# A sequence model's scan layers on one core: the skip term, the norm's factor, the ffn's buffer and the place of z

## The chip, the cores and the metric

The kernel runs on one core of a Trainium2 chip. The metric is the device time of one execution in microseconds, here the median of three runs. Five engines work in parallel, each through its own instructions in order: TensorE (PE), VectorE (DVE), ScalarE (ACT), GpSimd (POOL) and SyncE (SP), which in this kernel only issues transfers (DMAs).

## The reference

Four parts follow one another on an image `x` of 2 x 128 x 64 x 64; the change touches only the first, two scan layers over the 4096 positions of each image, all in fp32:

```python
t = embed(x)
for i in range(2):
    r = t
    u, z = split(layernorm(t) @ in_w.T)              # 256 channels each
    u = silu(causal_conv4(u) + conv_b)
    dt, Bm, Cm = split(u @ xproj_w.T, [8, 24])       # 8, 16 and 16 wide
    dt = softplus(dt @ dt_w.T + dt_b)
    # for every position, in order:
    #   h = exp(dt * A) * h + (dt * u) * Bm          # 256 x 16 states
    #   y = sum over the 16 states of h * Cm
    y = (y + u * ssm_D) * silu(z)                    # u * ssm_D: the skip term
    t = y @ mout_w.T + r
    r = t
    t = gelu(layernorm(t) @ ffn_w1.T + b1) @ ffn_w2.T + b2 + r
x = x + outc(t)
```

`layernorm(t)` is `(t - mean) * rsqrt(var + eps) * ln_g + ln_b` over the 128 channels. After it come two attention layers and a layer of features at several scales, which are left as they are.

## The kernel before, in words

A piece (`items[i]`) is 512 positions of one image in one layer; there are 2 images x 2 layers x 8 = 32. Channels lie on the 128 partitions. The 256 x 16 states of a piece are worked in 8 groups of 4 scans: in a group (`g`), 128 partitions hold 32 channels x 4 states, and each of the four scans (`m`) is 128 x 512. A scan takes one slot, so a piece has 32 slots.

The order of all engines is written out by hand. `slot(i, todo, t_)` emits, for every slot, the work of the scan: transfers that spread `dt` to a group's partitions three groups ahead (`spread_dt`, tile `dtb`, on SP), a product that spreads `dt*u` (`spread_dtu`, tile `pdu` in a single PSUM buffer, PE), `y_pair` (the sum over states of two groups, 32 small products on PE into `py`), the `scan` itself (DVE, line 430), `decay` four scans ahead (`da = exp(dt*A)`, ACT, line 419, four PSUM buffers), and at a group's end `times_b` (DVE, line 412, which reads `pdu` and fills the next `h`) and on GpSimd the carry (line 432) and `h * Cm` (line 433, `cb`). After that the slot emits what `background(i)` has listed for it with `at(slot, function, ...)`. That is everything else, for neighbouring pieces: with `i` the piece that is scanned, `n = i + 1`, `p = i - 1`, `q = i - 2`, `r = i + 2`,

- `pu_taps` and `pu_out` (convolved u of `n`), `xproj`, `spread_bc` (Bm and Cm to all groups through DRAM, tiles `dr`, `bb`, `cb`), `dtproj`, `soft_plus` (`dt`), `dt_end` (`dtu = dt * u`, GpSimd, line 393);
- `pz_mm`, `pz_out` (z of `i`), and `silu` of u of `n` with z of `i` at slot 11;
- `y_out` (the skip term, DVE, line 453), `gate` (times z, GpSimd, line 456), `mix_out`, `mix_add`;
- the norm for two pieces at once, the ffn's of `p` and the mixer's of `r`: `ln_centre` and `ln_square` (slots 12 to 15), `ln_var` (17), on 2 x 512 values `ln_eps` (18), `ln_rs` (19: Ln, Exp and Square on ACT), `ln_newton` (20: GpSimd, then ACT, line 298) and `ln_step` (21: GpSimd, line 302, the factor `rs` is done), `ln_spread` (27: a product with a row of ones spreads `rs` to 128 partitions, `pr`, line 306), `ln_scale` (28: DVE, line 310) and `ln_shift` (29: ACT, line 323, into `x2` or `xn`);
- `ffn_up` (slots 30 and 31, `ph`, line 478, and `hid`, line 479), `gelu`, `ffn_down`, `ffn_add`, `out_mm`, `out_add`.

An engine takes its instructions strictly in this order; the PSUM pool `mm` of two buffers serves all products but `pdu`, `py` and `da`. Before the first piece is scanned, the loop runs for `i = -2` and `i = -1`, which prepare pieces 0 and 1, and `load_rest` and `fold_out` issue large transfers there. The `h` tiles come from a ring of five buffers, which `hid` shares:

```python
w["hid"] = sp.tile([P, 4, CH], F32, name="hid", tag="h", bufs=5)
```

## Time and profile before

| | |
|---|---|
| median of 3 runs (lowest, highest) | 4975.6 us (4974.84, 4981.31) |
| profiled execution: its own time, its span | 4975.69 us, 4973.9 us |
| layers (the change's place) | from the start to about 2100 us |
| mean clock of PE that was granted | 0.949 over the span; 0.90 from 278 to 2051 us |
| DVE busy in the layers, a 200 us window (400 to 600) | 187.7 us |
| PE, ACT, GpSimd busy in the same window | 183.2, 146.6, 145.3 us |
| `dtb` of one quarter, 64 KB, issue to landing | 2.0 us |
| `cb` and `bb`, 256 KB each, four in a row, issue to landing | 4.6 and 4.5 us |

The profile counts an engine as busy while an instruction of its own runs; a matmul's end is modelled. A timeline row gives the start, the time from the first instruction's start to the last one's end, engine, line, operation, output and inputs, how many instructions were merged, and in brackets the idle time before it with what ended it. A row of groups gives the count, busy time and mean of one in ns, and then the idle time before the group with its releasers. An fp32 product of 128 x 512 is two matmul instructions in the records (x2). A window's row has length, then busy time (and instructions) of PE, PE's weight loads, DVE, ACT and GpSimd, then the granted clock, DMA's busy share and GB/s.

### The profile page before, as it was taken

The numbers are of one execution on the slowest core, as the hardware profiler recorded it, in microseconds if no ns is written. First come the engines' busy times: TensorE is split into PE (matmuls) and PEld (weight loads), VectorE is DVE, ScalarE is ACT, GpSimd is POOL, SyncE is SP. The second block draws the span as 40 slices with busy tenths as digits, with TensorE's granted clock in tenths as the row PEclk, the third lists the DMA queues.
The fourth block names the chain that finished last, engine by engine and source line by source line (L and its number), as shares of the span: only waits on it lengthen the run. The fifth ranks groups of instructions, "written<-read, shape, count | busy, mean of one in ns | idle before, by whom it ended". The sixth has DMA issues, their size and how long they took to land.

```text
span 4973.9 us, 48435 instructions
## 1 busy us (share of the span) xinstructions
PE 4643.1 (93%) x14634; PEld 2218.0 (45%) x14634; DVE 3975.5 (80%) x4155; ACT 2361.8 (47%) x3225; POOL 2331.1 (47%) x1974
## 2 busy tenths in 40 slices
PE   6899999999988899899999999999999999999997
PEld 2222222222222222266667766666666666333332
DVE  6999999999999999878886677767766775667775
ACT  4677777777777777632222232233333332323332
POOL 3777776676777777613332233333333332334231
PEclk8888898988999989899999999999999999999998
DMA  6333332223333333214444444444444443000000
GB/s 163 68 67 68 69 69 67 67 67 71 69 69 69 71 73 71 69 36 126 113 111 123 113 109 115 122 99 111 114 101 98 114 112 83 3 7 7 7 5 9
DMA packets 242485, 386.28 MB, mean 78 GB/s; under 512 B 88608, under 2 KB 89136, under 8 KB 233776
## 3 DMA queue, kind: packets, MB, share of 16 engines
q1 hardware_dynamic: 193072, 316.01, 26.1%
q10 hardware_dynamic: 49152, 67.17, 5.4%
q8 instruction: 117, 1.92, 0.2%
q14 instruction: 144, 1.18, 0.1%
HBM read 101.09 MB, written 13.37 MB: 23 GB/s over the span
## 4 chain that ended last, share of the span: by engine, by line
PE 46%; POOL 25%; issue 12%; DVE 8%; DMA 4%; SPq 3%; ACT 3%; ACTq 0%; POOLq 0%; DVEq 0%
POOL h L433 19%; PE pq L780 13%; PE po L830 13%; DVE tr L810 3%; SPq L821 3%; DMA pt<-tr 3%; PE pa L677 2%; PE pf L1135 2%; PE pqkv L1162 2%; PE pw L1221 1%; POOL dtu L393 1%; POOL z L456 1%; PE pb L677 1%; PE pfus L1286 1%; PE psc L1186 1%
## 5 line engine op out<-in xcount | busy, mean ns | idle before, releaser
L817 POOL COPY pt<-tr 32x512 f32<-32x512 f32 x1024 | 644.7, 630 | 1410.8 <-DVE tr L810 700.7
L430 DVE TENSOR_TENSOR_SCAN h<-da,carry,h 128x512 f32<-128x512 f32 x1024 | 1241.6, 1265 | 65.1 <-ACT da L419 36.2
L433 POOL TENSOR_TENSOR h<-h,cb 128x2048 f32<-128x2048 f32 x256 | 1160.9, 4535 | 20.8
L780 PE MATMUL pq<-k,q 128*128 128x512 f32 x2048 | 963.4, 593 | 12.5 <-DVE sc L785 12.5
L830 PE MATMUL po<-pt,vt 128*128 128x256 f32 x4096 | 965.6, 379 | 3.5 <-POOL pt L817 3.5
L795 ACT ACTIVATE sc<-sc,nm 128x2048 f32<-128x2048 f32 x256 | 510.5, 1995 | 886.8 <-DVE nm L791 656.4
L830 PEld LDWEIGHTS po<-pt,vt 128*128 128x128 f32 x4096 | 777.9, 190 | 309.5 <-issue 227.5
L785 DVE TENSOR_SCALAR_CACHE_REDUCE sc<-pq 128x1024 f32<-128x1024 f32 x512 | 624.8, 1222 | 333.8 <-PE pq L780 311.7
L419 ACT ACTIVATE da<-dtb,am 128x512 f32<-128x512 f32 x1024 | 681.4, 684 | 221.3 <-DVE h L430 205.6
L412 DVE TENSOR_TENSOR h<-bb,pdu 128x2048 f32<-128x2048 f32 x256 | 581.4, 2271 | 85.4 <-PE py L445 28.3
L810 DVE STREAM_TRANSPOSE tr<-sc 128x2048 f32<-128x2048 f32 x256 | 591.6, 2311 | 65.7 <-DMA pt<-tr 59.3
L445 PE MATMUL py<-h,sel 128*32 128x512 f32 x2048 | 513.6, 645 | 1.8 <-POOL h L433 1.8
L780 PEld LDWEIGHTS pq<-k,q 128*128 128x128 f32 x2048 | 382.2, 190 | 291.5 <-issue 247.4
L406 PE MATMUL pdu<-dtu,fsel 128*128 128x512 f32 x512 | 327.8, 727 | 99.5 <-DVE h L412 97.5
L445 PEld LDWEIGHTS py<-h,sel 128*32 128x32 f32 x2048 | 115.6, 118 | 418.7 <-issue 413.1
L333 PE MATMUL pu<-xn,wu 128*128 128x512 f32 x512 | 245.9, 614 | 10.0 <-ACT u L339 8.3
L406 PEld LDWEIGHTS pdu<-dtu,fsel 128*128 128x128 f32 x512 | 96.6, 215 | 307.4 <-DVE h L412 180.5
L432 POOL COPY carry<-h 128x4 f32<-128x4 f32 x256 | 47.8, 187 | 390.3 <-DVE h L430 386.2
L1228 DVE TENSOR_TENSOR ov<-v,pw 128x2048 f32<-128x2048 f32 x64 | 146.2, 2284 | 65.1 <-PE pw L1221 65.1
L1162 PE MATMUL pqkv<-f,ws 128*128 128x512 f32 x384 | 188.8, 617 | 3.0 <-DVE prod L1179 2.3
L1232 POOL TENSOR_TENSOR ov<-ov 128x2048 f32<-128x2048 f32 x16 | 72.6, 4536 | 237.0 <-DVE ov L1228 237.0
L393 POOL TENSOR_TENSOR dtu<-dt,u 128x1024 f32<-128x1024 f32 x32 | 75.1, 2348 | 199.1 <-ACT dt L387 199.1
(265 smaller groups left out, 5152.4 us busy)
## 6 DMA issues: line engine op xcount, KB each, us to landing
pt<-tr SPq DMA_DIRECT2D x2048, 64.0 KB, 2.0
dtb<-dt SPq DMA_DIRECT2D x1024, 64.0 KB, 2.0
pt<-tr ACTq DMA_DIRECT2D x1024, 64.0 KB, 2.1
bb<-dr SPq DMA_DIRECT2D x128, 256.0 KB, 4.5
cb<-dr SPq DMA_DIRECT2D x128, 256.0 KB, 4.6
uw<-ufold SPq DMA_DIRECT2D x12, 576.0 KB, 4.4
uw<-dkept SPq DMA_DIRECT2D x20, 288.0 KB, 3.1
xt<-in_x SPq DMA_DIRECT2D x16, 256.0 KB, 4.8
```

The source lines that it names most:

```text
L406: nc.tensor.matmul(pdu, lhsT=four(s_ % 4), rhs=st[i]["dtu"][:, s_ // 4, :], start=True, stop=True)
L412: nc.vector.tensor_tensor(h, st[i]["bc", 0], pdu.unsqueeze(1).to_broadcast([P, 4, CH]), ALU.mult)
L419: nc.scalar.activation(da, st[i]["dtb", s_], AF.Exp, scale=am[items[i][1]][:, j, gg, m : m + 1])
L430: nc.vector.tensor_tensor_scan(h[:, m, :], da, h[:, m, :], carries[b, l][:, j, gg, m : m + 1], ALU.mult, ALU.add)
L433: nc.gpsimd.tensor_tensor(h, h, st[i]["bc", 1], ALU.mult)
L445: nc.tensor.matmul(py[r : r + 32, :], lhsT=sel, rhs=st[i]["h", s_ + k][:, m, :], start=(m == 0), stop=(m == 3), tile_position=(0, r),)
L780: nc.tensor.matmul(pq[:, i, :], lhsT=sta["q", r, grp][:, it * P : (it + 1) * P], rhs=sta["k"][:, at : at + CH], start=True, stop=True)
L785: nc.vector.tensor_scalar(dst, pq, 1.0, None, ALU.mult, ALU.max, accum_out=sta["mx"][:, c2 : c2 + 1])
L795: nc.scalar.activation(sc, sc, AF.Exp, bias=nm, scale=scale, accum_out=sm[:, hh : hh + 1])
L810: nc.vector.transpose(tr, sta.pop(("sc", r, blk, hh)).rearrange("p (t r f) -> p r t f", r=NB, f=32))
L817: nc.gpsimd.tensor_copy(dst, src)
L830: nc.tensor.matmul(sta["po", r, grp], lhsT=sta["vt"][:, jt, :], rhs=rhs, start=(jt == 0), stop=(jt == N // P - 1))
```

## The change

1. The skip term becomes a product: `turn_skip` builds `ssm_D` as a diagonal matrix on GpSimd (at each new image and layer), `y_pair` starts the sum in `py` with it, and `y_out` is a copy on ACT.
2. The norm's factor: `ln_eps` joins `ln_rs`, `ln_step` joins `ln_newton`, both a slot earlier; `ve` and `nt` lie in rows of `sq`. The product that spread `rs` is replaced by a transfer to DRAM (`ln_out`, slot 21) and a broadcast transfer into `sq` (`ln_in`, slot 23), both on SP; `ln_scale` runs on GpSimd (slots 25 and 27), `ln_g` moves into `ln_shift` (slot 28).
3. `hid` has a buffer of its own outside the ring of `h`, and `xr` uses the buffer of `x2`.
4. z is computed a piece ahead, for `n` at slots 24 to 27 rather than for `i` at slots 1 to 6.

```diff
-        def ln_eps(w, n):
-            w["ve"] = spl.tile([2, CH], F32, name="ve", tag="ve")
-            nc.scalar.activation(w["ve"][:n], w.pop("var")[:n], AF.Identity, bias=eps[:n])
-
         def ln_rs(w, n):
-            w["rs"] = spl.tile([2, CH], F32, name="rs", tag="rs")
-            nc.scalar.activation(w["rs"][:n], w["ve"][:n], AF.Ln)
...
+            ve, nt = w["sq"][:n, 0, :], w["sq"][:n, 1, :]
+            rs = w["rs"] = spl.tile([2, CH], F32, name="rs", tag="rs")
+            nc.scalar.activation(ve, w.pop("var")[:n], AF.Identity, bias=eps[:n])
+            nc.scalar.activation(rs[:n], ve, AF.Ln)
+            nc.scalar.activation(rs[:n], rs[:n], AF.Exp, scale=-0.5)
+            nc.scalar.activation(nt, rs[:n], AF.Square)
 
         def ln_newton(w, n):
 
-            nt = w["nt"][:n]
-            nc.gpsimd.tensor_tensor(nt, nt, w["ve"][:n], ALU.mult)
+            ve, nt, rs = w["sq"][:n, 0, :], w["sq"][:n, 1, :], w["rs"][:n]
+            nc.gpsimd.tensor_tensor(nt, nt, ve, ALU.mult)
             nc.scalar.activation(nt, nt, AF.Identity, bias=c15[:n], scale=-0.5)
-
-        def ln_step(w, n):
-            rs = w["rs"][:n]
-            nc.gpsimd.tensor_tensor(rs, rs, w["nt"][:n], ALU.mult)
-
-        def ln_spread(w, k, n):
-            w["pr", k] = mmt("pr")
-            nc.tensor.matmul(w["pr", k], lhsT=pick(k, n), rhs=w["rs"][:n], start=True, stop=True)
-
-        def ln_scale(w, k, i):
+            nc.gpsimd.tensor_tensor(rs, rs, nt, ALU.mult)
+
+        def ln_out(w, n):
+            w["rd"] = dp.tile([2, CH], F32, name="rd", tag="rd")
+            nc.sync.dma_start(w["rd"][:n], w["rs"][:n])
+
+        def ln_in(w, n):
+            src = w["rd"][:n].rearrange("(o k) f -> o (k f)", o=1)
+            nc.sync.dma_start(w["sq"][:, :n, :].rearrange("p k f -> p (k f)"), src.to_broadcast([P, n * CH]))
+
+        def ln_scale(w, k):
             cen = w["cen"][:, k, :]
-            nc.vector.scalar_tensor_tensor(cen, cen, vl("ln_g", i), w.pop(("pr", k)), ALU.mult, ALU.mult)
+            nc.gpsimd.tensor_tensor(cen, cen, w["sq"][:, k, :], ALU.mult)
...
-            nc.scalar.activation(dst, w["cen"][:, k, :], AF.Identity, bias=vl("ln_b", i))
+            nc.scalar.activation(dst, w["cen"][:, k, :], AF.Identity, bias=vl("ln_b", i), scale=vl("ln_g", i))
...
-                st[i]["py", j] = yp.tile([P, CH], F32, name="py", tag="y")
+                py = st[i]["py", j] = yp.tile([P, CH], F32, name="py", tag="y")
+                nc.tensor.matmul(py, lhsT=skip["now"][:, j, :], rhs=st[i]["u"][:, j, :], start=True, stop=False)
...
+        def turn_skip(i):
+            if items[i][2] == 0:
+                dg = skip["now"] = wp.tile([P, NJ, P], F32, name="skip", tag="skip")
+                for j in range(NJ):
+                    nc.gpsimd.tensor_tensor(dg[:, j, :], ident, vl("ssm_D", i, j).to_broadcast([P, P]), ALU.mult)
+
         def y_out(i, j):
-            u = st[i]["u"][:, j, :]
-            nc.vector.scalar_tensor_tensor(u, u, vl("ssm_D", i, j), st[i].pop(("py", j)), ALU.mult, ALU.add)
+            nc.scalar.copy(st[i]["u"][:, j, :], st[i].pop(("py", j)))
...
-                if i == NI - 1:
-                    w["hid"] = spa.tile([P, 4, CH], F32, name="hid", tag="sc", bufs=3)
-                else:
-                    w["hid"] = sp.tile([P, 4, CH], F32, name="hid", tag="h", bufs=5)
+                w["hid"] = spl.tile([P, 4, CH], F32, name="hid", tag="hid")
...
-                xr = st[i]["xr"] = spl.tile([P, CH], F32, name="xr", tag="xr")
+                xr = st[i]["xr"] = spl.tile([P, CH], F32, name="xr", tag="x2")
...
+                at(24, pz_mm, n, 0), at(25, pz_out, n, 0)
+                at(26, pz_mm, n, 1), at(27, pz_out, n, 1)
             if has(i):
-                at(1, pz_mm, i, 0), at(3, pz_out, i, 0)
-                at(5, pz_mm, i, 1), at(6, pz_out, i, 1)
+                at(2, turn_skip, i)
...
-                at(27, ln_spread, w, k, m), at(28, ln_scale, w, k, it)
-                at(29, ln_shift, w, k, it, second)
+                at(25 + 2 * k, ln_scale, w, k)
+                at(28, ln_shift, w, k, it, second)
             if pair:
-                at(17, ln_var, w, m), at(18, ln_eps, w, m), at(19, ln_rs, w, m), at(20, ln_newton, w, m), at(21, ln_step, w, m)
+                at(17, ln_var, w, m), at(18, ln_rs, w, m), at(19, ln_newton, w, m)
+                at(21, ln_out, w, m), at(23, ln_in, w, m)
```

More of the change, by code (lines that the diff above doesn't have):

```diff
@@ L144, in tile_conv_seq @@
         load_x(0, 0)
-        wl, wu, wd, am, cws = [], [], [], [], []
+        wl, wu, wd, am, cws, skip = [], [], [], [], [], {}
         def load_layer(l):
@@ L281, in ln_var @@
                 nc.tensor.matmul(var[:n], lhsT=kc[:, at : at + n], rhs=w["sq"][:, k, :], start=(k == 0), stop=(k == n - 1))
-        def ln_eps(w, n):
-            w["ve"] = spl.tile([2, CH], F32, name="ve", tag="ve")
-            nc.scalar.activation(w["ve"][:n], w.pop("var")[:n], AF.Identity, bias=eps[:n])
         def ln_rs(w, n):
-            w["rs"] = spl.tile([2, CH], F32, name="rs", tag="rs")
-            nc.scalar.activation(w["rs"][:n], w["ve"][:n], AF.Ln)
-            nc.scalar.activation(w["rs"][:n], w["rs"][:n], AF.Exp, scale=-0.5)
-            w["nt"] = spl.tile([2, CH], F32, name="nt", tag="nt")
-            nc.scalar.activation(w["nt"][:n], w["rs"][:n], AF.Square)
+            ve, nt = w["sq"][:n, 0, :], w["sq"][:n, 1, :]
@@ L445, in y_pair @@
                     nc.tensor.matmul(
-                        py[r : r + 32, :], lhsT=sel, rhs=st[i]["h", s_ + k][:, m, :], start=(m == 0), stop=(m == 3),
+                        py[r : r + 32, :], lhsT=sel, rhs=st[i]["h", s_ + k][:, m, :], start=False, stop=(m == 3),
                         tile_position=(0, r),
                     )
+        def turn_skip(i):
[3 more added lines that the diff above has]
+                    nc.gpsimd.tensor_tensor(dg[:, j, :], ident, vl("ssm_D", i, j).to_broadcast([P, P]), ALU.mult)
         def y_out(i, j):
-            u = st[i]["u"][:, j, :]
-            nc.vector.scalar_tensor_tensor(u, u, vl("ssm_D", i, j), st[i].pop(("py", j)), ALU.mult, ALU.add)
+            nc.scalar.copy(st[i]["u"][:, j, :], st[i].pop(("py", j)))
         def gate(i):
```

## The prediction

> **What bounds the kernel now.** I read the page first: engine shares, then the slices.

> ```profile
> PE 4643.1 (93%) x14634; PEld 2218.0 (45%) x14634; DVE 3975.5 (80%) x4155; ACT 2361.8 (47%) x3225; POOL 2331.1 (47%) x1974
> DVE  6999999999999999878886677767766775667775
> PEclk8888898988999989899999999999999999999998
> ```

> The layers fill the first 17 slices; only there does the change act. DVE is full and PE looks full at a clock below one, so neither is yet the answer. I then took 28 whole pieces (from one start of `gate`, line 456, to the 28th after it) by windows, and DVE's groups in that stretch.

> ```profile
> 278.24:2051.38 1773.14, 1609.90 (x4088) 489.76 (x4087) 1650.43 (x1232) 1303.93 (x1840) 1256.55 (x591) 0.90 0.31 70
> ```

> ```profile
> L430 DVE TENSOR_TENSOR_SCAN h<-da,carry,h 128x512 f32<-128x512 f32 x897 | 1087.6, 1265 | 51.7 <-ACT da L419 25.8 <-POOL carry L428 3.6 <-ACT hid L479 1.5
> L412 DVE TENSOR_TENSOR h<-bb,pdu 128x2048 f32<-128x2048 f32 x224 | 508.8, 2271 | 71.0 <-PE py L445 26.3 <-PE pdu L406 19.7 <-issue 13.0
> L453 DVE SCALAR_TENSOR_TENSOR u<-u,vec,py 128x512 f32<-128x512 f32 x56 | 41.0, 732 | 0.0
> L310 DVE SCALAR_TENSOR_TENSOR cen<-cen,vec,pr 128x512 f32<-128x512 f32 x55 | 38.0, 730 | 0.0
> ```

> A piece takes 1773.14/28 = 63.3 us: DVE works 58.9 (57.0 in scan and product, 2.8 in the two steps that leave, less overlap) and waits 4.4. That invites "2.8 off DVE, 2.8 off the piece". The timeline of one piece (735 to 799 us) says otherwise. PE:

> ```profile
> 745.94 1.13 PE L406 MATMUL pdu<-dtu,fsel 128*128 128x512 f32 x2
> 748.93 3.62 PE L306 MATMUL pr<-rs,kc 2*128 2x512 f32 x4 [1.86 <-POOL rs L302]
> 754.02 2.07 PE L406 MATMUL pdu<-dtu,fsel 128*128 128x512 f32 x2 [1.47 <-DVE h L412]
> 756.02 5.27 PE L445 MATMUL py<-h,sel 128*32 128x512 f32 x16
> 761.23 3.89 PE L478 MATMUL ph<-x,wl 128*128 128x512 f32 x8
> ```

> From `pdu` of slot 28 (691.1 in the piece before, 754.0 in this one) to `pdu` of slot 16 (ended 735.5) PE runs 44.4 us without a gap, and DVE waits for it there. From 735.5 to 754.0 (18.5 us) PE waits, and a chain through ACT, GpSimd and DVE sets the time. The piece is the sum of the two. GpSimd, ACT and SP in that second part, and a small transfer's time to land (the last figure of its row):

> ```profile
> 738.47 2.35 POOL L393 TENSOR_TENSOR dtu<-dt,u 128x1024 f32<-128x1024 f32 x1 [5.47 <-ACT dt L387]
> 741.03 4.54 POOL L433 TENSOR_TENSOR h<-h,cb 128x2048 f32<-128x2048 f32 x1
> 745.54 1.26 POOL L297 TENSOR_TENSOR nt<-nt,ve 2x512 f32<-2x512 f32 x1
> 747.63 1.25 POOL L302 TENSOR_TENSOR rs<-rs,nt 2x512 f32<-2x512 f32 x1 [0.83 <-ACT nt L298]
> 749.09 4.51 POOL L433 TENSOR_TENSOR h<-h,cb 128x2048 f32<-128x2048 f32 x1
> 753.82 4.53 POOL L433 TENSOR_TENSOR h<-h,cb 128x2048 f32<-128x2048 f32 x1
> ```

> ```profile
> 746.83 0.72 ACT L298 ACTIVATE nt<-nt,c 2x512 f32<-2x512 f32 x1 [2.61 <-POOL nt L297]
> 747.46 3.88 ACT L419 ACTIVATE da<-dtb,am 128x512 f32<-128x512 f32 x6
> ```

> ```profile
> 742.18 1.92 SPq L377 DMA_DIRECT2D cb<-dr  x4
> ```

> ```profile
> dr<-dbl SPq DMA_DIRECT2D x20, 64.0 KB, 1.6
> ```

> GpSimd runs 738.5 to 758.3 with one gap of 0.8 us: it is full exactly where the change gives it two more products.

> **The change, part by part** (us of one piece; D = 738.4, when `dt` is done; the lines are those of the kernel before).

> *Skip term, its sum to ACT.* Off DVE: two of 0.73. On PE: two products of 0.86 to 0.95 at full clock, like a `pdu`. The one at slot 12 (with groups 0, 1) lies in PE's full stretch: +0.9. The one at slot 28 falls where the windows show the clock at 0.51 (749 to 756) and 0.58 (756 to 760), where one `pdu` takes 2.07: +0.9 to +1.9. ACT gets two copies of 0.59 in gaps of its own: `py` is finished before them (745.9, against 747.46 and later). The diagonal is built four times in all, two small products on GpSimd in a gap of over 2 us: 0, or some 3 us in all without the gap. `gate` now waits for ACT's copy where it waited for DVE's step: 0.

> *z a piece ahead.* Two products (1.9) leave PE's full stretch for slots 24 and 26, where PE waits anyway; two copies go along on ACT, behind decays that run ahead. -1.9, which the two skip products take back.

> *ffn's values in their own buffer.* `hid` no longer takes a place in the ring of five `h`, so `times_b` doesn't wait for `y_pair` at slot 7: 26.3 us over 28 pieces, at most 0.9 each. In a stretch that PE fills this wait only moves to the next `pdu`: I count 0. `xr` in the buffer of `x2` is loaded at slot 9, long after `ph` has read `x2`: 0.

> *Newton a slot earlier.* ACT is in order. Line 298 waits for GpSimd (2.61 us) and now stands ahead of the decay of slot 20 and behind Ln, Exp and Square, which stand ahead of the decay of slot 19. So scan 24, which ran at 745.36, waits for its `da`: 746.8 + 0.7 + 0.65 = 748.1. Four scans (4.8) and `times_b` (2.36) then end at 755.3 rather than 754.0: +1.3, the 0.72 of line 453 already taken off.

> *Norm's factor by transfers and GpSimd.* Two `pr` (3.6, in PE's waiting time: worth 0) and two DVE steps (1.4) go. In their place, in order:
> - `rs` is done at D + 10.5, as before (GpSimd's order up to it is unchanged).
> - SP waits for it with `ln_out`. Queued behind that wait are the four `cb` (1.05 MB), which were issued at 742.18 (D + 3.8) and now go at D + 10.9, then `ln_in` (512 KB broadcast, waiting also for `ln_out` to land: 1.6, from `dr`, while `cb` moves), then the `dtb` of slots 24 and 28, which have some 16 us to spare.
> - The windows show 207 GB/s from 742 to 749. `cb` and `ln_in` are 1.57 MB: 7.6 us from D + 11.7, so `ln_in` lands at about D + 19.3 (757.7). Bounds: 15.5, if 512 KB overtook `cb`, and 21.5 at the slowest full window (156 GB/s).
> - GpSimd is free at D + 15.2 (753.6) and stands before `ln_scale` of slot 25 until D + 19.3. Behind it: 1.2 for the scale (half of a `dtu`, 2.35), 4.8 for carry and `h` of group 6, 1.2 for the second scale: D + 26.4.
> - ACT at slot 28 waits for both with `ln_shift`: D + 27.1. Behind it two decays (1.25) and `hid` (0.65): D + 29.0.
> - PE can make two `ph` by then, not the third, as `mm` has two buffers: third and fourth `ph` and the next `pdu` end at D + 31.8.
> - From there to `pdu` of slot 16 it was 33.6 (701.9 to 735.5); less 1.9 for z, plus 0.9 for the skip, less 0.4 for what a mean piece has less of embed and output products: 32.2.
> - From that `pdu` to `dt` it was 2.9; ACT's own chain from `mix_add` is unchanged while the skip product moves `pdu` back 0.9, so 2.0 to 2.9.

> Sum: 31.8 + 32.2 + 2.0 to 2.9 = 66.0 to 66.9 against 63.3. This is a new ring (dt, norm, transfer, GpSimd, ACT, PE), 2.7 to 3.6 longer; some 29 pieces go round it: +78 to +104, of which I take 85.

> *The start.* `ln_out` at 21.3 us stands behind loads (`wo`, issued at 18.5, took 7.3 to land), `ln_in` comes after it, `load_rest` behind both: `xn` about 31 rather than 25: +6. In the next round `ln_in` stands behind `cb` and the six 576 KB writes of `fold_out`, and ACT's shift with the decays of scans 1 to 3 behind that; they had run while DVE waited 5.1 us for `dtb`: +4 to +7. Together +11. *The end* (last piece; nothing else in the queue): 0 to +4, taken as 0.

> Profiled execution 4975.7 (span 4973.9 and 1.8 around it; the median of the three runs is 4975.6): 4975.7 + 85 + 11 = **5072**.

> [...]

> **Rivals.**
> 1. *The transfer lands in time* (before D + 15.2; `ln_in` alone would take 2.5). Then the third `ph` doesn't wait. What remains is the +1.3 of Newton, the skip at the low clock, and up to 0.9 off: 64.1 to 65.0 a piece, +23 to +49, with the start 5010 to 5036. Against: `cb` goes ahead of it in one queue.
> 2. *Faster: DVE's relief counts.* It decides if, besides landing in time, PE's stretch is warm from slot 28 (z gives PE work at slots 24 and 26). `pdu`, skip, `y_pair`, four `ph` and `pdu` then take 9.8 instead of 12.8: 61.2 to 62.1, -35 to -61 and the start: 4926 to 4952. DVE's work alone (57.0 and 0.9 of gaps) would allow 4830. Against: from the end of z's products (750) PE still stands some 5 us before slot 28, and a 2.9 us wait now is already followed by half clock.
> 3. *No net effect*: ring and relief cancel, within 10 us.

> **How the numbers follow.** The ring is what I forecast: 0.63, with 5030 to 5140 by the bounds of the landing (2 us a piece is 58). Rival 1 0.15, rival 2 0.18, rival 3 0.04. This kernel's measurement can tell about 0.2% (10 us) from no change. Faster 0.18, same 0.04, slower 0.78. The range 4968 to 5145 leaves out rival 2 and little above; the ring's own range is 5030 to 5140.

> **What would show it.** Right: GpSimd idle about 4 us before the scale on a DMA; `ph` waiting for ACT `hid`; scans waiting for ACT about 3 us at slots 20 and 33; DVE's idle time up from 4.4 to 9 us a piece; pieces of 66. Wrong: GpSimd not idle before the scale (rival 1), PEclk near 1.0 and DVE over 95% busy (rival 2), or `ln_in` landing within 5 us of `rs`.

## The result, and the profile after

The changed kernel takes 5102.5 us (median of 4 runs, 5098.5 to 5110.6) against 4977.3 us for the kernel before on the same chip: a ratio of 1.0253 [1.0235, 1.0271], 125 us slower. Forecast were 5072 us and a range of 4968 to 5145.

The start times of `gate` cut the span into three parts. Between the first and the 31st start lie 30 pieces.

| us | before | after | difference |
|---|---|---|---|
| up to the first `gate` | 150.15 | 162.94 | +12.8 |
| 30 pieces | 1901.2 (63.37 each) | 2005.6 (66.85 each) | +104.4 |
| the rest of the span | 2922.5 | 2928.1 | +5.6 |
| span | 4973.9 | 5096.7 | +122.8 |

The page of the kernel after, engine shares, then DVE's and the clock's slices:

```profile
PE 4611.0 (90%) x14634; PEld 2235.6 (44%) x14634; DVE 3902.6 (77%) x4027; ACT 2396.3 (47%) x3289; POOL 2407.9 (47%) x2046
DVE  5888888888888888878887677767766776667776
PEclk8899999999989989899999999999999999999998
```

DVE's nines of the first 17 slices are eights now: it has 73 us less to do and waits more. The clock of PE did not get worse (0.92 in the row below, 0.90 in that of before). Twenty-eight whole pieces, by windows, and the scans among DVE's groups in that stretch:

```profile
298.05:2168.56 1870.51, 1580.08 (x4089) 502.59 (x4088) 1583.50 (x1121) 1334.01 (x1897) 1324.36 (x651) 0.92 0.32 74
```

```profile
L428 DVE TENSOR_TENSOR_SCAN h<-da,carry,h 128x512 f32<-128x512 f32 x897 | 1089.9, 1268 | 215.4 <-ACT da L417 173.8 <-POOL carry L426 21.6 <-DVE h L410 0.5
```

DVE works 56.6 us a piece and idles 10.2 (before 58.9 and 4.4): 2.4 us of work left, and 5.8 us of waiting came. In the 28 pieces the scans' wait for ACT's decays alone rose from 25.8 to 173.8 us, and all idle time before scans from 51.7 to 215.4. What holds up the scans, ACT, GpSimd and PE, in the waits of the same stretch (total, times, longest):

```profile
DVE h L428 <- ACT da L417: 173.8, 134, 3.6
ACT xn L321 <- POOL cen L308: 123.9, 24, 5.2
POOL cen L308 <- DMA sq<-rd: 107.6, 28, 4.9
PE ph L479 <- ACT hid L480: 67.1, 27, 3.6
```

Read from the third line up: GpSimd stands 3.8 us a piece before the scale until the broadcast has landed, ACT stands 5.2 us before the shift until GpSimd has scaled, and scans and the ffn's products wait for what is queued behind that shift on ACT. (Part of the scans' wait has another cause, in `Ln`, `Exp` and `Square` a slot earlier; see the part on the prediction.) The chain of waits through one piece (start, length, what) is the new ring itself; `dt` is done at 784.3, which is D:

```profile
784.39 2.34 POOL dtu L391
...
791.44 1.27 POOL sq L294
...
796.95 5.97 DMA sq<-rd
...
802.99 1.26 POOL cen L308
...
804.46 1.98 POOL h L431
...
808.96 1.28 POOL cen L308
...
810.26 0.81 ACT xn L321
...
812.27 0.62 ACT hid L480
...
812.93 1.98 PE ph L479 x4
814.91 0.86 PE pdu L404 x2
```

The transfer holds the chain for 6 us before the first scale; the second scale stands behind a product of 4.5 us on GpSimd, and ACT's shift behind both. The last `pdu` of this chain opens PE's full stretch. In SP's queue the four `cb` stand between the transfer that writes `rs` to DRAM and the broadcast that reads it back:

```profile
794.81 0.23 SPq L300 DMA_DIRECT2D rd<-rs  x1
795.09 1.70 SPq L375 DMA_DIRECT2D cb<-dr  x4
796.95 0.34 SPq L304 DMA_DIRECT2D sq<-rd  x1
```

### The profile page after: what moved, and what is told of

Its sections match the earlier page's. It is cut to its first block, busy times and chain, and to the rows that moved or that the text cites. A ratio compares the mean times of both kernels' runs of the same rounds, so it can differ in the third digit from the quotient of the medians.

```text
span 5096.7 us, 48529 instructions
## 1 busy us (share of the span) xinstructions
PE 4611.0 (90%) x14634; PEld 2235.6 (44%) x14634; DVE 3902.6 (77%) x4027; ACT 2396.3 (47%) x3289; POOL 2407.9 (47%) x2046
## 3 DMA queue, kind: packets, MB, share of 16 engines
q1 hardware_dynamic: 198240, 332.92, 26.4%
q8 instruction: 117, 1.92, 0.2%
## 4 chain that ended last, share of the span: by engine, by line
PE 50%; POOL 14%; issue 11%; DVE 8%; DMA 7%; ACT 6%; SPq 3%; ACTq 0%; DVEq 0%; POOLq 0%
PE pq L783 12%; PE po L833 12%; POOL h L431 9%; PE pu L331 4%; DMA sq<-rd 3%; DVE tr L813 3%; ACT da L417 3%; DMA pt<-tr 3%; SPq L824 3%; PE py L444 2%; PE pa L680 2%; PE pf L1138 2%; PE pqkv L1165 2%; POOL cen L308 1%; POOL dtu L391 1%
## 5 line engine op out<-in xcount | busy, mean ns | idle before, releaser
L428 DVE TENSOR_TENSOR_SCAN h<-da,carry,h 128x512 f32<-128x512 f32 x1024 | 1243.8, 1268 | 253.3 <-ACT da L417 191.9
L444 PE MATMUL py<-h,sel 128*32 128x512 f32 x2048 | 489.0, 620 | 5.2 <-POOL h L431 5.2
L479 PE MATMUL ph<-x,wl 128*128 128x512 f32 x256 | 133.6, 647 | 73.5 <-ACT hid L480 73.5
L1231 DVE TENSOR_TENSOR ov<-v,pw 128x2048 f32<-128x2048 f32 x64 | 146.2, 2285 | 63.5 <-PE pw L1224 63.5
```

Source lines behind the costliest of these rows:

```text
L428: nc.vector.tensor_tensor_scan(h[:, m, :], da, h[:, m, :], carries[b, l][:, j, gg, m : m + 1], ALU.mult, ALU.add)
L444: nc.tensor.matmul(py[r : r + 32, :], lhsT=sel, rhs=st[i]["h", s_ + k][:, m, :], start=False, stop=(m == 3), tile_position=(0, r),)
```

## The experiments

The theory: the time goes into this ring, whose length is set by the place of the broadcast behind `cb` in SP's queue and by GpSimd's order; DVE's relief is worth nothing. Rivals: the skip products on PE or ACT's copies cost the time; Newton's step a slot earlier costs it; or the ring would have been harmless but for one of its parts. Times are medians, ratios stand against the kernel before run in the same rounds (4976.2 to 4977.7 us).

**1 and 2. The change in two halves.** First the norm alone on the kernel before (`ln_rs` to `ln_shift` and their slots as after; skip, `hid` and z as before); then all the rest with the norm of before:

```diff
 # 2, on the kernel after; ln_eps to ln_shift and their slots as before, and
-            w["ve"] = spl.tile([2, CH], F32, name="ve", tag="ve")
+            w["ve"] = w["sq"][:, 0, :]
-            w["nt"] = spl.tile([2, CH], F32, name="nt", tag="nt")
+            w["nt"] = w["sq"][:, 1, :]
```

> Only the norm's part of the change, on the kernel before. Theory (the ring dt, rs, transfers behind cb, GpSimd, ACT, third ph, PE sets the piece): the whole loss is here and z's two products are back in PE's full stretch, so the piece is 67 to 68 us and the time 5100 to 5135; GpSimd stands about 3.5 us a piece before the scale on the transfer. Rival A (Newton's wait a slot earlier on ACT is the whole cost, 1.3 us a piece, and the transfers are hidden): 5010 to 5035. Rival B (the two skip products on PE and ACT's copies cost it): 4950 to 4990.

Measured: 5170.3 us, 1.0383 [1.0366, 1.0400], pieces of 69.32. The norm alone costs 193 us, more than the whole change and 35 us above the theory's range. The ring is the expected one, but PE, which has no z products in its waiting time here, pays for it twice. After its wait for `hid` the next two `ph` run at about half speed (timeline; four instructions took 1.98 just before, from 906.28, at a clock of 1.00). They are slowed in 19 of the 24 pieces from 300 to 1990 us; in the kernel after it is 5 of 25:

```profile
910.90 3.58 PE L476 MATMUL ph<-x,wl 128*128 128x512 f32 x4 [2.63 <-ACT hid L477]
```

And `times_b` waits 82.0 us in all for `py` (300 to 1990 us; 23.9 in the kernel before). With `hid` late, its place in the ring of `h` would come free late; whether that is the reason was not tried by itself.

> All parts but the norm's: skip product, ffn's own buffer, z a piece ahead; the norm's factor is spread by a product and scaled on VectorE as before, with ve and nt kept in rows of sq to make room. Theory: no ring through transfers, PE's stretch keeps its length (two skip products for two z products), the wait for y_pair is gone: 0 to 1 us a piece less, 4945 to 4980. Rival A: the same. Rival B: 5060 to 5110, since the skip products remain.

Measured: 4994.1 us, 1.0031 [1.0021, 1.0041], pieces of 63.78: a miss by 14 us at the upper end. The rest gains nothing (it costs 16 us); runs 7 to 10 take it apart. One thing shows at once: PE's `pr` of the norm, which the kernel after no longer has, now waits for ACT's copies of z (timeline):

```profile
752.63 1.09 PE L306 MATMUL pr<-rs,kc 2*128 2x512 f32 x2 [2.88 <-ACT z L349]
```

**3. The second `cb` ahead of the norm's transfers in SP's queue.**

```diff
 # on the kernel after
-at(14, spread_bc, n, 0), at(22, spread_bc, n, 1)
+at(14, spread_bc, n, 0), at(20, spread_bc, n, 1)
```

> The changed kernel with cb issued at slot 20, ahead of the transfer that writes rs, rather than at slot 22 behind it. Theory: the broadcast no longer stands behind 1 MB; it lands about 3 us earlier, GpSimd's wait before the first scale falls from 3.8 to under 1 us a piece, the piece to 64 to 65 us, the time to 5010 to 5050. Rival A (Newton): no change, 5095 to 5110. Rival C (GpSimd's two more products and their place before h, not the transfer, are the cost): under 15 us gained, 5085 to 5110.

Measured: 5013.0 us, 1.0069 [1.0054, 1.0084], pieces of 64.19. One slot number takes back 90 of the 125 us. SP now issues `cb` 7 us ahead of the norm's transfers, GpSimd waits 0.62 rather than 3.48 us for the broadcast (at D + 15.9), and the four pairs of `ph` run without a gap (timeline):

```profile
763.90 1.92 SPq L375 DMA_DIRECT2D cb<-dr  x4
770.75 0.23 SPq L300 DMA_DIRECT2D rd<-rs  x1
772.08 0.34 SPq L304 DMA_DIRECT2D sq<-rd  x1
776.09 1.26 POOL L308 TENSOR_TENSOR cen<-cen,sq 128x512 f32<-128x512 f32 x1 [0.62 <-DMA sq<-rd]
785.38 3.89 PE L479 MATMUL ph<-x,wl 128*128 128x512 f32 x8
```

**4. Newton's step back to the slots of before.**

```diff
 # on the kernel after; ln_eps a function of its own again
-at(17, ln_var, w, m), at(18, ln_rs, w, m), at(19, ln_newton, w, m)
+at(17, ln_var, w, m), at(18, ln_eps, w, m), at(19, ln_rs, w, m), at(20, ln_newton, w, m)
```

> The changed kernel with eps, Ln/Exp/Square and Newton back at slots 18, 19, 20; everything else as changed. Theory: rs is done at the same time after dt, so the ring keeps its length; DVE's wait at scan 23 shrinks but it waits elsewhere: within 10 us of the changed kernel, 5090 to 5110. Rival A: 1.3 us a piece comes back, 5060 to 5070.

Measured: 5130.8 us, 1.0304 [1.0288, 1.0319], pieces of 67.94: 28 us slower than after, where the theory had about no change and the rival a gain. The ring is as long as before the edit (third `ph` at D + 28.8). PE starts the `pdu` of slot 28 1.2 us earlier after D, is through with the first two `ph` 2.2 us earlier, and so stands longer before the third `ph` (timeline), and the clock falls behind that gap. Two windows of this kernel, the gap and what follows it (the clock is the third figure from the end):

```profile
825.79 2.66 PE L481 MATMUL ph<-x,wl 128*128 128x512 f32 x4 [3.71 <-ACT hid L482]
```

```profile
822.00:826.00 4.00, 0.28 (x2) 0.21 (x2) 1.45 (x2) 2.87 (x5) 3.92 (x4) 1.00 0.00 0
826.00:830.00 4.00, 4.00 (x7) 1.53 (x7) 2.21 (x2) 3.09 (x6) 3.58 (x3) 0.62 0.23 51
```

In the piece of the kernel after that is shown above, the same wait is 1.27 us, the shortest but one, and the four `ph` instructions take 1.98. Over all pieces from 300 to 1990 us the wait is 2.5 us on average there and 3.7 here, and the two `ph` behind it are slowed in 5 of 25 pieces there and in 21 of 25 here. From the start of the third `ph` to the end of the next `pdu` it is 3.2 us on average there and 4.5 here; the piece is 1.1 longer. So here, with the ring closed by the transfer, being early on PE only made the wait longer (3.7 us against 2.5), and behind the longer wait the two `ph` were slowed in 21 of 25 pieces rather than 5.

**5 and 6. Both edits, then both scales at slot 25 as well.**

```diff
 # 5 is 3 and 4 together; 6 is 5 with
-                at(25 + 2 * k, ln_scale, w, k)
+                at(25, ln_scale, w, k)
```

> The changed kernel with both edits: cb issued ahead at slot 20, and eps, Ln/Exp/Square and Newton back at slots 18, 19, 20. Theory: with the broadcast out of the way the third ph no longer waits for ACT, so the wait of scan 23 for its decay (2.7 us in the run with cb ahead) is what is late; taking it away gives 1.0 to 1.5 us a piece against that run: 4968 to 4985, about the kernel before. Rival D (Newton's place costs nothing by itself, as its move back alone gave a loss of 28 us): 5005 to 5020 or slower.

Measured: 4988.7 us, 1.0026 [1.0015, 1.0037], pieces of 63.46, 4 us above what the theory allowed and well below its rival. With the transfer out of the way the same Newton edit that cost 28 us gains 24.

> The same, and both scales on GpSimd at slot 25, ahead of h of group 6, rather than one before and one behind it. Theory: xn is ready 4.8 us earlier, but with cb ahead nobody waits for it any more; h of group 6 comes 1.3 us later into slack: within 8 us of the run with cb and Newton moved. Rival E (ACT's wait at slot 28 for the second scale still holds back the decays): 15 to 40 us faster than that run.

Measured: 4970.9 us, 0.9989 [0.9980, 0.9998], pieces of 62.83. The rival held: the second scale, which stood behind a 4.5 us product on GpSimd, was the last link. The wait of ACT's shift for GpSimd falls from 113.4 us (run 5, 300 to 1990 us) to 1.3. Both scales run in one go (timeline):

```profile
759.68 2.49 POOL L310 TENSOR_TENSOR cen<-cen,sq 128x512 f32<-128x512 f32 x2 [0.85 <-DMA sq<-rd]
```

**7 and 8. The ffn's buffer with z a piece ahead, without skip and norm; then z four slots earlier.**

```diff
 # 7: the kernel before with hid in its own buffer, xr in that of x2, ve and nt in rows of sq, z as after
 # 8: 7 with
-                at(24, pz_mm, n, 0), at(25, pz_out, n, 0)
-                at(26, pz_mm, n, 1), at(27, pz_out, n, 1)
+                at(20, pz_mm, n, 0), at(21, pz_out, n, 0)
+                at(21, pz_mm, n, 1), at(22, pz_out, n, 1)
```

> The kernel before with only the ffn's buffer and z a piece ahead at slots 24 to 27 (ve and nt in rows of sq to make room); no skip product, norm as before. Theory: PE's full stretch loses two products (1.9 us) and DVE loses the wait for y_pair; the spread products then wait up to 0.5 us for ACT's copy of z: 1.2 to 1.7 us a piece, 4925 to 4942. Rival F (DVE's own work bounds the kernel, so z's place is worth nothing): 4965 to 4978.

> As the run before with z's products at slots 20 and 21 and its copies at 21 and 22, so that the norm's spread products don't wait for the copies. Theory: up to 0.5 us a piece better than at slots 24 to 27: 4912 to 4935. Rival F: 4965 to 4978.

Measured: 4933.8 us, 0.9917 [0.9904, 0.9931], pieces of 62.08 for the first; 4921.3 us, 0.9891 [0.9878, 0.9905], pieces of 61.65 for the second, as expected both. In run 7 the `pr` products wait 69.8 us for ACT's z copies and their weight loads 42.8 (300 to 1990 us). In run 8 no product waits for them, and the weight loads wait 11.8. Run 8 is the fastest of all versions.

**9 and 10. The ffn's buffer alone, the skip term alone.**

```diff
 # 9, on the kernel before (xr in the buffer of x2; ve and nt in rows of sq)
-                    w["hid"] = sp.tile([P, 4, CH], F32, name="hid", tag="h", bufs=5)
+                w["hid"] = spl.tile([P, 4, CH], F32, name="hid", tag="hid")
 # 10, on the kernel before: turn_skip, y_pair and y_out as after
```

> The kernel before with the ffn's buffer alone (hid in a place of its own; xr in the place of x2; the norm's ve and nt in rows of sq). Theory (the prediction's count of nothing for this step): 4966 to 4986 us, a piece of 63.3 to 63.5. Rival H (the buffer, not z, is what made the kernel with both 43 us faster, since the h ring gets a place back): 4930 to 4950 us, a piece of 62.0 to 62.6. If the buffer alone is slower, over 4990, then z a piece ahead is worth more than the 1.3 us a piece that the two gave together.

Measured: 4976.6 us, 1.0000 [0.9992, 1.0009], pieces of 63.29. The buffer is worth nothing here. `times_b` waited 23.9 us for `py` and 18.6 for `pdu` in the kernel before (300 to 1990 us); now it waits 60.0 us for `pdu`: the wait moved to the next product. So the gain of run 7 is z's, unless the two act only together: z alone was not run.

> The kernel before with the skip term alone: two diagonal products a piece on TensorE, the y sums copied by ScalarE, the diagonals made by GpSimd once a layer. Theory (the prediction's 1.8 to 2.8 us a piece, brought down to the 1.7 that the runs with and without it differ by): 1.2 to 2.8 us over 30 pieces, 5012 to 5062 us, likeliest 5028. Rival S (the difference between those two runs came from the z copies and the y copies meeting on ScalarE at slots 24 to 28, and the products hide in TensorE's waits): 4974 to 4998 us.

Measured: 5016.8 us, 1.0080 [1.0067, 1.0092], pieces of 64.57: +1.20 a piece, the lower end of the theory's range. The product of slot 28 falls behind a PE that has just waited, and takes 1.82 us where the one of slot 12 takes 1.02 (timeline):

```profile
766.52 2.07 PE L406 MATMUL pdu<-dtu,fsel 128*128 128x512 f32 x2 [2.97 <-DVE h L412]
768.39 1.82 PE L441 MATMUL py<-u,skip 128*128 128x512 f32 x2
```

**11. What seemed best of all parts:** the norm of run 6, buffer and z of run 8, the skip term on DVE.

```diff
 # run 8's kernel with ln_rs to ln_shift as in run 6, cb's second part at slot 20, and
-                at(27, ln_spread, w, k, m), at(28, ln_scale, w, k, it)
+                at(25, ln_scale, w, k)
```

> The norm by transfers and GpSimd with the cb transfer issued at slot 20, Newton's step at the slots of before and both scales at slot 25; the ffn's buffer; z a piece ahead at slots 20 and 21; the skip term as in the kernel before, on VectorE. Theory (parts add up: 4971 for this norm with skip and z at 24 to 27, less 51 for the skip products, less 12 for z's slots): 4890 to 4925 us, a piece of 60.3 to 61.4, so no slower than the 4921 of the kernel with the norm of before. Rival F (a shorter piece opens the norm's ring again, since its length from dt to the ffn stays at some 27 us: TensorE waits for hid anew): 4926 to 4960 us, with over 1 us of ph's wait for ScalarE in a piece.

Measured: 4936.1 us, 0.9914 [0.9901, 0.9928], pieces of 61.75. The time lies in the rival's range, its reason does not hold: `ph` waits for nothing (timeline). Against run 8 the piece is the same within 0.1 us, although DVE has lost two steps of it and PE two products. The 15 us are the start (first `gate` at 159.3 against 147.0 us) and 30 times that 0.1.

```profile
690.01 2.05 PE L406 MATMUL pdu<-dtu,fsel 128*128 128x512 f32 x2 [4.46 <-DVE h L412]
690.20 2.49 POOL L310 TENSOR_TENSOR cen<-cen,sq 128x512 f32<-128x512 f32 x2 [0.74 <-DMA sq<-rd]
697.56 3.89 PE L475 MATMUL ph<-x,wl 128*128 128x512 f32 x8
```

From `dt` to the first `ph` it is 23.3 us here (674.2 to 697.6), 23.0 in run 8, 22.8 in the kernel before. Taking `pr` off PE made its wait before `pdu` longer (4.46 us; 1.89 in the piece of run 8 at 674.7) and the chain no shorter.

## Why the prediction was right, and where it was off

*What bounds the kernel: right.* The piece is PE's full stretch and a waiting part that a chain of four engines sets. Run 11 tests "2.8 off DVE is not 2.8 off the piece" for the norm's half: with 1.4 us moved from DVE to GpSimd and the transfer in time, the piece moved by 0.1 us, the wrong way.

*The ring: right, link by link.* In the piece whose chain is shown above:

| step | predicted | measured |
|---|---|---|
| `rs` done | D + 10.5 | D + 10.5 |
| broadcast landed, scale starts | D + 19.3 (15.5 to 21.5; by its own 156 GB/s the upper bound is 21.8) | D + 18.7 |
| second scale done | D + 26.4 | D + 25.9 |
| shift done | D + 27.1 | D + 26.8 |
| `hid` done, third `ph` starts | D + 29.0 | D + 28.6 |
| `pdu` ends | D + 31.8 | D + 31.5 |
| from there to `pdu` of slot 16 | 32.2 | 32.3 |
| from there to `dt` | 2.0 to 2.9 | 2.8 |

With `cb` out of the way it was D + 15.9 (run 3), near the lower bound of 15.5. The signs it named came: the idle time before the scale 3.8 us a piece (4 foretold), `ph` waiting for `hid`, scans waiting for decays, DVE's idle time 10.2 (9), pieces of 66.85 (66). One of them came at another place: the long wait, 2.91 us, is that of the scan of slot 23, for a decay queued behind `Ln`, `Exp` and `Square` (they waited 0.97 us for PE's `var`), and not that of slot 24 behind line 298; slot 33 waits 1.74 us where about 3 were named. The scan of slot 24 itself, which the prediction had at D + 9.7, started at D + 9.8: the right time by another link.

*Prices of the ring.* The scale on GpSimd, taken at 1.2, took 1.26 against DVE's 0.73; for 128 x 2048 GpSimd's 4.54 stand against the 2.27 of `times_b` on DVE. For the small write the prediction took 1.6, from `dr`; SP's 4 KB write had landed 1.3 us after its issue in run 3, when SP issued the read that waits for it (770.75 and 772.08).

*The term that was mis-sized: +85 for the ring, measured +104.* The bounds were 78 to 104, from 66.0 to 66.9 a piece. The forecast took the value nearer the lower one, +2.9 for 29 pieces; it was +3.48 for 30. The piece shown sums to 66.6; its last step, left open between 2.0 and 2.9, was 2.8, and that is the term that the choice had set too low. The mean piece is 0.3 longer than the one shown. The start, foretold +11, was +12.8, though not by the parts: the first `xn` came 4.0 us later (28.2 against 24.2), not 6, the second round took the rest. The end was +5.6 where 0 to +4 stood. Together 19 + 2 + 6 = 27 of the 30 us by which 5072 was low; the profiled execution lay 4 us below the median.

*Newton a slot earlier, +1.3: too much, and only without the wait for the transfer.* The prediction's sum of the ring does not hold this term; its rival 1 does. Run 4 shows that inside a closed ring it costs nothing, even less than nothing (taking it out lost 28 us); runs 3 and 5 show 0.73 us a piece where the ring is open.

*Skip.* Predicted were +1.8 to +2.8 on PE. The 0.72 of DVE's step in the waiting part, which the prediction takes off under Newton, leaves 1.1 to 2.1. Alone it is +1.20 (run 10); beside z at slots 24 to 27 it is 1.70 (run 2 less run 7). The low clock at slot 28 was right: 0.50 from 766 to 770 us in run 10 (windows), and 1.82 against 1.02 us for the product.

*z and the buffer.* The buffer's 0 was exact (run 9). z was to bring -1.9 a piece, as its products move to PE's waiting time; at slots 24 to 27 it brought 1.3 on the norm of before, and 1.7 at slots 20 and 21, where the `pr` products do not stand behind ACT's copies.

*The rivals.* Rival 1, "the transfer lands in time", gave 5010 to 5036 us for a kernel whose transfer is early; run 3 is that kernel, at 5013. It was the right price for a condition that did not hold. Rival 2, DVE's relief, asked besides for a PE that is warm from slot 28, at full clock. No run had that: a `pdu` takes 1.02 us at a clock of 1.00 (kernel after, 814.75), and that of slot 28 takes 2.04 us in the piece shown of the kernel after and 2.05 in those of runs 3 and 11; from 300 to 1990 us it is that slow in all but two of the pieces of these three. So its condition failed and its price was not tested; run 11 only shows that the norm's half of the relief is worth nothing without it. Its argument that a wait of 2.9 us is followed by half clock reads the trace in the wrong order: in that piece of the kernel before, the wait ran from 688.2 to 691.1, and the clock had fallen from 1.00 to 0.50 at 687.7. Rival 3, no net effect, is excluded by the 125 us.

*What stays open.* The parts taken alone (norm +193, skip +40, buffer 0; buffer with z -43) sum to +190, the whole change is +125. The half clock behind PE's wait is part of the difference: from the third `ph` to the end of the next `pdu` it is 4.42 us on average in run 1 and 3.20 in the kernel after, over 30 pieces an estimated 37 of the 65 us. The place of `hid` in the ring of `h` may be part of the rest; neither was taken alone from the norm of after.

## What to carry over

Before moving work from a full engine to one with idle time on average, look at the stretch in which it will run: here GpSimd, 47% busy over the span, was nearly full there, and the moved 1.4 us of DVE work bought a wait of 3.8 us on GpSimd and 5.2 on ACT. The time of the transfer that entered the chain here went with its place in SP's queue (8.2 us from `rs` to the scale behind `cb`, 5.4 with `cb` issued ahead); the first edit to try is the order of that queue (one slot number was worth 90 us). The move that filled an engine's waiting time with its own later work (z, -1.3 to -1.7 us a piece) paid; the one that only shortened an engine's work (1.4 us off DVE, run 11 against run 8) did not.

## What the runs showed of the hardware

```profile
811.60:813.00 1.40, 0.13 (x2) 0.07 (x1) 1.31 (x2) 1.40 (x4) 1.40 (x1) 1.00 0.00 0
813.00:815.00 2.00, 2.00 (x5) 0.98 (x6) 2.00 (x2) 1.77 (x4) 2.00 (x1) 1.00 0.00 0
...
767.50:769.80 2.30, 0.03 (x3) 0.00 (x1) 2.24 (x2) 1.13 (x2) 1.47 (x2) 1.00 0.84 175
769.80:771.00 1.20, 1.20 (x3) 0.67 (x4) 1.00 (x1) 1.20 (x3) 1.12 (x3) 1.00 0.01 0
...
908.30:909.50 1.20, 0.00 (x0) 0.00 (x0) 1.10 (x2) 1.20 (x2) 1.12 (x3) 1.00 0.00 0
909.50:910.90 1.40, 0.00 (x1) 0.00 (x1) 1.40 (x2) 1.40 (x4) 1.40 (x1) 0.94 0.00 0
910.90:912.50 1.60, 1.60 (x2) 0.83 (x3) 1.60 (x3) 1.10 (x2) 1.60 (x1) 0.50 0.00 0
...
823.50:825.70 2.20, 0.00 (x0) 0.00 (x0) 1.15 (x1) 2.20 (x5) 2.20 (x1) 1.00 0.00 0
825.70:827.00 1.30, 1.21 (x3) 0.67 (x4) 1.30 (x3) 1.24 (x4) 1.30 (x1) 0.99 0.00 0
827.00:828.30 1.30, 1.30 (x3) 0.40 (x2) 1.21 (x2) 0.64 (x1) 0.97 (x2) 0.50 0.19 43
...
687.00:688.50 1.50, 0.00 (x0) 0.00 (x0) 1.50 (x2) 1.50 (x3) 1.50 (x1) 1.00 0.99 298
688.50:690.00 1.50, 0.00 (x0) 0.02 (x1) 1.40 (x2) 0.10 (x1) 0.95 (x1) 0.76 0.64 216
690.00:692.00 2.00, 1.99 (x4) 0.50 (x4) 2.00 (x2) 0.72 (x2) 1.80 (x2) 0.50 0.45 107
```

If the clock fell once in each of the windows with 0.94, 0.99 and 0.76, it fell 2.5 us after the wait began in run 1, 4.9 in run 4, where PE had been back at work for 1.2 us, and 3.7 in run 11 (an estimate from these means). The length of the wait alone does not tell the cases apart: in the kernel before, the clock fell at 687.7 us, ahead of a wait, when PE had been busy for 2.70 of the last 3.40 us:

```profile
684.20:687.60 3.40, 2.70 (x8) 0.96 (x6) 3.40 (x4) 3.40 (x6) 2.81 (x3) 1.00 0.40 82
687.70:691.00 3.30, 0.48 (x1) 0.00 (x0) 3.30 (x3) 1.38 (x2) 3.22 (x3) 0.50 0.39 89
```

What sets the moment of the fall was not shown.

The broadcast of 512 KB and the 4 KB that it depends on took 5.4 us from `rs` to the scale where `cb` had been issued 7 us before them (run 3: 770.7 to 776.1) and 8.2 us behind 1 MB of `cb` (after: 794.8 to 803.0).
